# Start order, narrower causal masks and a holding rule in a two-layer attention and feed-forward kernel

## The chip, the cores and the metric

The kernel runs on one core of a Trainium2 chip. The metric is device time in microseconds; three runs of the kernel before gave 1493.4, 1504.54 and 1507.78 us, median 1504.54. The engines are TensorE (PE, with its weight loads as PEld), VectorE (DVE), ScalarE (ACT), GpSimd (POOL) and SyncE (SP), which issues the DMAs.

## The reference

x is 8 batches of 512 tokens with 256 channels; ctx_512 is 8 x 512 x 128. Two layers follow one another. Each has an attention with 16 heads of 16 channels and a quantised feed-forward network of width 1024, and each adds its result to x:

```python
x = x + _L0_xattn_ref(_layernorm(x), ctx_512, ...)   # causal self-attention + cross-attention, one output product
x = x + _L0_ffn_ref(_layernorm(x), ...)              # rmsnorm, 8-bit activations per token, ternary weights, GELU
x = x + _L1_xattn_ref(_layernorm(x), ctx_512, ctx_512, ...)   # cross-attention
x = x + _L1_ffn_ref(_layernorm(x), ...)              # 8-bit activations and weights, one scale per tensor, GELU
```

The causal part is the one that the masks belong to:

```python
att = jnp.einsum('bhqd,bhkd->bhqk', q, k) * scale
causal = jnp.tril(jnp.ones((T, T), bool))
att = jnp.where(causal[None, None], att, -jnp.inf)
y = jnp.einsum('bhqk,bhkd->bhqd', jax.nn.softmax(att, axis=-1), v)
```

## The kernel before

**The work and its tiles.** The attention is cut into 24 units (`UNITS`, L36): for each batch an S unit (causal self-attention), a C unit (cross-attention of layer 0) and an X unit (cross-attention of layer 1). A unit has four groups G of four heads, so there are 96 groups. Every group goes through three series of steps:

- `max_one` (L632): scores with queries on partitions, 48 rows of q and k (three parts, which make up one product with the precision of two) into a pair of PSUM banks; for S units the causal mask is added by `masks` (L615); VectorE takes the row maxima (`mx`).
- `exp_one` (L720): the scores again, with keys on partitions and two more rows (the row maxima, and ones), so that the maximum is already subtracted; for S units again `masks`; ScalarE takes the exponential into a tile `p`.
- `av_part` (L768): p times v into one bank, four heads in four column strips of the array (32 columns each).

In an S unit a score step has one or two query tiles (L49, L51), and each of these has one 128 x 128 block on the diagonal. `masks` adds NEG to what lies above it by two products per array half c (64 rows each), k = 0 and 1: identity times mask for the maxima, mask times identity for the exponentials, each over all 128 columns of a block. For two blocks a product has 256 columns.

**What prepares the groups.** `ln_job` (L477) loads x, takes its statistics on VectorE, normalises it (for the first batch on VectorE, else on GpSimd) and turns it on TensorE into `xlt`. `weights_job` (L414) loads the query and key weights (`raw`) and reorders their columns (`w_Sq`, `w_Sk` and so on); the tag "oc" has two buffers. `prep_job` (L529) multiplies by them; ScalarE adds the bias from `qk_bias` (tile `qkt`), and the high and the low part of each value are split (for n < 2 on VectorE, else on GpSimd). `stack_job` (L566) copies the parts by six DMAs from `qkt` into the stacked rows of `qk`. `rows_job` (L670) turns the maxima into rows, `mrow`, and puts them into `qk` by DMA. `vprep_job` (L586) makes v. `init_job` (L1324) writes the rows of ones into `qk` and the ones that belong to v. `inputs_jobs` (L1350) runs `ln_job` and `ctx_job` in the order of the units.

**The order of the work.** It is set when the program is built. `Plan` (from L78) keeps a clock for each engine, with a cost for each operation: a TensorE product of so many columns by `pe` (L104, 0.008 us + columns/2340), a switch between tile modes by `SWITCH` (0.165). The modes are "rows" (scores, two row halves), "cols" (four column strips: values, projections, transposes) and "full". The main loop (from L1411) knows at each step which of the three series can go on: m (maxima), e (exponentials), a (values). A series is urgent if the backlog that the plan sees on its engine is under `FEED` (L223: in rows mode 9.0 us for VectorE, 2.2 for ScalarE; in cols mode 1.0 and 1.0). Urgent steps come first, then jobs by `run_jobs` (L197), then a value product, then any other step. So in rows mode, as soon as no score step is ready, a value product or a job's product is taken, and TensorE changes its mode. `evacuate` (L368) copies a bank to SBUF by ScalarE, if that ends in the plan no later than on VectorE plus `DVE_HANDICAP` (L228, 0.3 us). All engines then run this order as written, with semaphores; the profile shows what the chip makes of it. The helper lines L241 and L259 record nearly every VectorE and ScalarE operation and every matmul, so groups are told apart by their tiles.

**The start before.** In the program's order SyncE issues the eight DMAs of the doubled identity and mask (L356), the first weight (L421), eight of `qk_bias` (L426), x (L483), six of the rows of ones (L1332), and then the other weights.

Of the kernel before, what the change touches and what calls it, by code (L numbers as in the profile page):

```python
# [7 lines left out]
F32 = mybir.dt.float32  # L8
# [3 lines left out]
AF = mybir.ActivationFunctionType  # L12
# [64 lines left out]
class Plan:  # L77
# [26 lines left out]
    def pe(self, cols, mode="full"):  # L104

        if mode != self.mode:
            self.clock["pe"] += SWITCH
            self.mode = mode
        self.clock["pe"] += 0.008 + cols / 2340
        return self.clock["pe"] + PE_OUT - LAT  # L110

    def would(self, kind, n, *deps):
# [110 lines left out]
FEED = {"rows": (9.0, 2.2), "cols": (1.0, 1.0), "full": (1.4, 1.4)}  # L223
PATIENCE = {"rows": -5.0, "cols": -5.0, "full": -5.0}
GQ, AHEAD = 4, 3
ROW_COLS = 600
H1, H2 = {}, {}
DVE_HANDICAP = 0.3  # L228


class Readers:
# [55 lines left out]
def build(tc, A, out):  # L287
# [57 lines left out]
    with tc.tile_pool(name="start_b", bufs=1) as start:  # L345
        ident_b = start.tile([P, P], BF16, name="ident_b")
        nc.vector.tensor_copy(ident_b, ident)
        mask_b = start.tile([P, P], BF16, name="mask_b")
        nc.gpsimd.memset(mask_b, 0.0)
        nc.gpsimd.affine_select(  # L350
            mask_b, mask_b, pattern=[[-1, P]], compare_op=ALU.is_ge, fill=NEG, base=0, channel_multiplier=1,
        )
        for dst, of in ((ident2, ident_b), (mask2, mask_b)):
            for c in range(2):
                for k in range(2):
                    nc.sync.dma_start(dst[64 * c : 64 * c + 64, k], of[64 * k : 64 * k + 64])  # L356
    qk_bias = wp.tile([P, 6, 2], F32, name="qk_bias")

# [53 lines left out]
        WT[nm] = wp.tile([P, 1 if nm in ("Vc", "Vx") else 2, C], F32, name=f"w_{nm}")  # L412

    def weights_job():  # L414
        b6 = A["qk_bias"].rearrange("(g c d h) i u -> g c h d (i u)", g=2, c=2, h=2)
        for n, nm in enumerate(("Sq", "Sk", "Cq", "Ck", "Xq", "Xk")):
            for u in range(2):
                nk = WT[nm].shape[2]
                yield from take("oc")
                raw = tile("oc", [P, T], F32, f"raw_{nm}{u}")[:, : nk * P]  # L420
                nc.sync.dma_start(raw, WSRC[f"{nm}{u}"])  # L421
                t = dma(64 * nk)
                if n == 0 and u == 0:
                    for c, g, h in ((c, g, h) for c in range(2) for g in range(2) for h in range(2)):
                        p0 = 64 * c + 2 * g + h
                        nc.sync.dma_start(qk_bias[p0 : 64 * c + 64 : 4].rearrange("p i u -> p (i u)"), b6[g, c, h])  # L426
                        dma(6)
                yield t + LAT
                for k in range(nk):
                    for h in range(2):  # L430
                        full = raw[:, k * P : (k + 1) * P].rearrange("p (g c d h) -> p h c d g", g=2, c=2, h=2)
                        dst = WT[nm][:, u, k].rearrange("p (c d g h) -> p h c d g", c=2, g=2, h=2)
                        (nc.vector if n < 2 else nc.gpsimd).tensor_copy(dst[:, h], full[:, h])
                        t = plan.run("dve" if n < 2 else "pool", 0.2)
                give("oc", t)
                at["w", nm, u] = t
            if n == 1:
# [39 lines left out]
    def ln_job(key, src, nm, n_uses):  # L477

        if key[0] == "X":
            yield from until(("x3", key[1]))  # L480
        yield from take("xa")
        x = tile("xa", [P, NT, C], F32, f"xa_{nm}")
        nc.sync.dma_start(x, src())  # L483
        yield dma(512) + LAT
# [44 lines left out]
    def prep_job(n):  # L529
        kind, b = UNITS[n // 2]  # L530
        u = n % 2
        yield from take("qkt")
        tt = tile("qkt", [P, 4, T], F32R, f"qkt{n}")
        tl = []
        for i, (hi, lo) in enumerate(((0, 1), (3, 2))):
            wname, which = KIND[kind][i]
            key, ring = src_key(kind, b, which)
            yield from until(key, ("w", wname, u))
            xs = xlt[key]
            nk = xs.shape[1]  # L540
            ps, pb = yield from gen_bank()
            for k in range(nk):
                yield pe_next()
                wide(ps, WT[wname][:, u, k], xs[:, k, :], k == 0, k == nk - 1)
                tm = plan.pe(4 * T, "cols")
            used(key, ring, tm)
            bias = qk_bias[:, BIDX[wname], u : u + 1]
            full = tt[:, lo, :].bitcast(F32)
            nc.scalar.activation(full, ps, AF.Identity, bias=bias)
            t = op("act", T + 110, tm)  # L550
            give_bank(pb, t)
            yield t + LAT
            if n < 2:
                nc.vector.tensor_copy(tt[:, hi, :], full)
                th = op("dve2", T, t)
                nc.vector.tensor_tensor(tt[:, lo, :], full, tt[:, hi, :].bitcast(F32), ALU.subtract)
                tl.append(op("dve", T))
            else:
                copy_ts(tt[:, hi, :], full)
                th = op("pool", T, t)  # L560
                low_part(tt[:, lo, :], full, tt[:, hi, :])
                tl.append(op("pool2", T, th))
        qkt_t[n] = (tt.bitcast(F32), tl)
        at["qkt", n] = max(tl[0], th)

# [46 lines left out]

    mx_t = {}

    def masks(ps, c, blocks, lhs, rhs):  # L615

        n = len(range(*blocks.indices(NT)))
# [14 lines left out]
    def max_one(s):  # L632
# [21 lines left out]
        if kind == "S":  # L654
# [1 line left out]
            first = size[0] // P - 1  # L656
            step = size[-1] // P
            for c in range(2):
                masks(ps[:, c], c, slice(first, first + (len(qts) - 1) * step + 1, step), ident2, mask2)
# [60 lines left out]
    def exp_one(s):  # L720
# [25 lines left out]
        if kind == "S":  # L746
            step = (T - kts[0] * P) // P
            for c in range(2):
                masks(ps[c], c, slice(0, (len(kts) - 1) * step + 1, step), mask2, ident2)
# [18 lines left out]
    def av_part(s):  # L768
# [7 lines left out]
        for kt in kts:  # L776
            for j in range(4):
# [633 lines left out]
    while plan.jobs or a < len(AV_STEPS):  # L1411
# [279 lines left out]
```

## Time and profile before

| what | value |
|---|---|
| median of three runs | 1504.54 us |
| the profiled execution's own time | 1499.04 us |
| its span, first to last instruction | 1497.3 us |
| mean granted TensorE clock | 0.979 |
| weight loads of score products (two groups) | 152.1 and 146.3 us |
| maxima, all forms x768 | 809.5 us |
| exponentials, all forms x1408 | 715.8 us |
| value products x3072 | 363.9 us |
| mask products of exponentials, of maxima, x768 each | 65.6 and 65.1 us |
| DMA mean rate | 138 GB/s |

The profile's page gives busy times per engine, their course in 40 slices of the span (a digit is the busy share in tenths), the waits, and groups of instructions with count, busy time, mean duration in ns and the idle time before them. The timeline gives start, length, engine, line, operation and count, and in brackets the idle time before an instruction with what ended it. A busy time of TensorE is an envelope over pipelined products, so rates are read from start to start. Idle time of an engine that nothing waits for costs nothing.

### The profile page before, as it was taken

The page shows a single profiled execution, that of the slowest core. Times are in us where ns is not written, and L with a number is a line of the kernel's source. Part 1 is how long each engine was busy: PE and PEld are TensorE (multiplying, and loading weights), DVE is VectorE, ACT ScalarE, POOL GpSimd, SP SyncE. Part 2 cuts the span into 40 slices and gives each one's busy share as a digit, 9 for nine tenths or more (in the row PEclk, how much of TensorE's full clock was granted, in tenths as well). Part 3 has the DMA queues.
Part 4 walks back from the last instruction along what each step waited for, and adds up shares of the span by engine and source line. Part 5 has one row for each costly group of instructions (what it writes and reads, how often), then busy time and mean ns, then how long its engine had stood idle before and what let it go on. Part 6 is the DMA issues. An engine that isn't in the chain of part 4 may idle for free. (4 is left out here: it accounts for less than half of the span.)

```text
span 1497.3 us, 36194 instructions
## 1 busy us (share of the span) xinstructions
PE 1382.0 (92%) x14414; PEld 593.3 (40%) x14416; DVE 1194.1 (80%) x1723; ACT 1023.2 (68%) x1862; POOL 670.6 (45%) x928
## 2 busy tenths in 40 slices
PE   3899999999999999999999999999999989999768
PEld 1443444444433443443344334344333333333427
DVE  2787688788786897798876988698888978894597
ACT  1266667757757767767876677758778767778585
POOL 1552254464462455445634543555355533413237
PEclk9999999999999999999999999999999999999899
DMA  4854565576664666566549564757556656652343
GB/s 112 188 152 97 131 137 123 137 144 170 144 143 107 153 145 129 130 139 155 125 115 164 156 138 104 162 126 175 132 114 162 157 126 174 150 153 95 142 108 113
DMA packets 155612, 207.03 MB, mean 138 GB/s; under 512 B 71940, under 2 KB 74244, under 8 KB 154932
## 3 DMA queue, kind: packets, MB, share of 16 engines
q1 hardware_dynamic: 155444, 204.73, 56.9%
q8 instruction: 113, 1.85, 0.5%
q14 instruction: 55, 0.45, 0.1%
HBM read 68.15 MB, written 47.43 MB: 77 GB/s over the span
## 5 line engine op out<-in xcount | busy, mean ns | idle before, releaser
L241 DVE TENSOR_REDUCE mx<-pair 128x2 f32<-128x1024 f32 (+3 forms) x768 | 809.5, 1084 | 194.0 <-PE pair L259 186.9
L241 ACT ACTIVATE p<-bank 128x512 f32<-128x512 f32 (+1 forms) x1408 | 715.8, 585 | 271.5 <-PE bank L259 265.1
L259 PE MATMUL bank<-p,v 128*32 128x512 f32 (+3 forms) x3072 | 363.9, 551 | 2.6 <-ACT p L241 1.2
L259 PE MATMUL bank<-qk 50*128 50x512 f32 (+3 forms) x1536 | 331.1, 433 | 21.7 <-ACT p L241 9.5
L259 PE MATMUL pair<-qk 48*128 48x512 f32 (+3 forms) x1536 | 322.7, 431 | 24.8 <-DVE mx L241 14.1
L259 PEld LDWEIGHTS bank<-qk 50*128 50x128 f32 x1536 | 152.1, 186 | 279.1 <-ACT p L241 162.2
L259 PEld LDWEIGHTS pair<-qk 48*128 48x128 f32 x1536 | 146.3, 187 | 222.0 <-DVE mx L241 108.3
L366 POOL TENSOR_SCALAR qkt<-qkt 128x512 fp32r<-128x512 f32 x92 | 57.6, 626 | 277.9 <-ACT qkt L241 191.7
L391 POOL TENSOR_TENSOR qkt<-qkt 128x512 fp32r<-128x512 f32 x92 | 117.6, 1279 | 7.7
L241 ACT ACTIVATE qkt<-bank,qk_bias 128x512 f32<-128x512 f32 x96 | 66.5, 693 | 71.0 <-PE bank L259 51.0
L259 PEld LDWEIGHTS bank<-p,v 128*32 128x32 f32 x3072 | 69.8, 109 | 106.8 <-issue 80.2
L847 POOL TENSOR_TENSOR yt<-oc,rb 128x512 f32<-128x512 f32 x31 | 40.0, 1292 | 71.5 <-DMA rb<-scrz 59.1
L259 PE MATMUL bank<-ident,mask 64*128 64x128 bf16 (+1 forms) x768 | 65.6, 240 | 0.0
L259 PE MATMUL pair<-mask,ident 64*128 64x128 bf16 (+1 forms) x768 | 65.1, 243 | 0.0
L241 DVE SCALAR_TENSOR_TENSOR h<-bank,so,bc_l_b 128x512 f32<-128x512 f32 x64 | 45.7, 741 | 3.0 <-PE bank L259 1.4
L241 ACT ACT_TABLE_LOAD x34 | 43.6, 1283 | 3.1 <-DVE h L241 1.7
L1152 POOL TENSOR_SCALAR h<-h,sh 128x1024 f32<-128x1024 f32 x32 | 35.9, 1121 | 20.5 <-DVE sh L241 20.5
L1134 POOL TENSOR_SCALAR ms<-ms 128x2 f32<-128x2 f32 x16 | 3.1, 191 | 93.2 <-ACT jq L241 92.7
L241 ACT COPY ev<-bank 128x512 f32<-128x512 f32 x54 | 32.3, 599 | 14.8 <-PE bank L259 14.7
L395 POOL TENSOR_SCALAR hq<-h 128x1024 bf16<-128x1024 f32 x32 | 33.4, 1044 | 18.5 <-DMA hqt<-hq 13.0
L259 PE MATMUL bank<-l0w,hqt 128*32 128x256 bf16 x1024 | 37.9, 274 | 2.6 <-DMA hqt<-hq 1.7
L1591 POOL TENSOR_SCALAR g<-g,sc_g 128x2048 f32<-128x2048 f32 x11 | 29.4, 2690 | 22.2 <-DVE sc_g L241 22.2
(230 smaller groups left out, 1711.0 us busy)
## 6 DMA issues: line engine op xcount, KB each, us to landing
qk<-qkt SPq DMA_DIRECT2D x288, 256.0 KB
scro<-ev SPq DMA_DIRECT2D x94, 256.0 KB
oc<-scro SPq DMA_DIRECT2D x47, 256.0 KB
rb<-scrz SPq DMA_DIRECT2D x47, 256.0 KB
x_d<-xb SPq DMA_DIRECT2D x15, 512.0 KB
xa_s<-in_x SPq DMA_DIRECT2D x8, 512.0 KB
xb<-in_x SPq DMA_DIRECT2D x8, 512.0 KB
xr<-x_d SPq DMA_DIRECT2D x16, 256.0 KB
```

Of the source, the lines that this page charges most:

```text
L241: r = f(*args, **kw)
L259: r = self.eng.matmul(out, *args, **kw)
L366: nc.gpsimd.tensor_scalar(dst, src, 1.0, 0.0, ALU.mult, ALU.add)
L391: nc.gpsimd.tensor_tensor(dst, full, high.bitcast(F32), ALU.subtract)
L395: nc.gpsimd.tensor_scalar(dst, src, -MAGIC, 1.0, ALU.add, ALU.mult)
L847: nc.gpsimd.tensor_tensor(y, o, rb, ALU.mult)
L1134: nc.gpsimd.tensor_scalar(ms, ms, 1.0 / FF, 1e-5, ALU.mult, ALU.add)
L1152: nc.gpsimd.tensor_scalar(ht, ht, s[:, t - t0 : t - t0 + 1], MAGIC, ALU.mult, ALU.add)
L1591: nc.gpsimd.tensor_scalar(gs, gs, sg[:, 1:2], MAGIC, ALU.mult, ALU.add)
```

## The change

It has five parts.

1. **Start.** The first x and the first halves of Sq and Sk are loaded by the first three DMAs of the program, ahead of the constants. The bias comes next, then the doubled identity and mask. The weights are taken in the order Sq0, Sk0, Sq1, Sk1. The V and output weights, the rows of ones with v's ones, and the inputs of all later units wait until the plan has stacking 0 landed. In preparations 0 and 1 both products are issued before either is split.
2. **Masks.** For the maxima the second product (k = 1) covers columns 64 to 128 only; for the exponentials product k covers columns 64k to 64k + 64 only. The weights of these products stay 64 x 128.
3. **Order rule.** In rows mode, with nothing urgent, the loop looks for an m or e step whose inputs come ready within `LINGER` = 0.2 us; if there is one, the plan's TensorE clock is moved to it, and no value product is taken before.
4. **Evacuations.** `DVE_HANDICAP` goes from 0.3 to 0.8 us.
5. **The plan's costs.** A product in cols mode costs the larger of columns/2415 and columns/2165 - 0.08; mask products and value products have new column counts.

```diff
-        self.clock["pe"] += 0.008 + cols / 2340
+        self.clock["pe"] += max(cols / 2415, cols / 2165 - 0.08) if mode == "cols" else 0.008 + cols / 2340
...
+LINGER = 0.2
...
-DVE_HANDICAP = 0.3
+DVE_HANDICAP = 0.8
...
+    first_x = tile("xa", [P, NT, C], F32, "xa_s0")
+    nc.sync.dma_start(first_x, A["x"][0])
+    at["x0"] = dma(512)
+    heapq.heappop(plan.rings["xa"])
+    first_raw = {}
+    for i, nm in enumerate(("Sq", "Sk")):
+        first_raw[nm] = tile("oc", [P, T], F32, f"raw_{nm}0")
+        heapq.heappop(plan.rings["oc"])
+        nc.sync.dma_start(first_raw[nm][:, :C], A["wa"][2 * i])
+        at["raw", nm] = dma(128)
...
+        order = [(nm, u) for nm in ("Sq", "Sk", "Cq", "Ck", "Xq", "Xk") for u in range(2)]
+        order[:4] = [("Sq", 0), ("Sk", 0), ("Sq", 1), ("Sk", 1)]
...
+            if n == 3:
+                yield from until(("stack", 0))
                 for v in ("Vs", "Vc", "Vx", "Wp", "Wo"):
...
+            ready.append((wname, ps, pb, tm, hi, lo))
+            if n >= 2 or i == 1:
+                for r in ready:
+                    th = yield from split(*r)
+                ready = []
...
         for k in range(2):
+            lhs, rhs = (mask2, ident2) if keys else (ident2, mask2)
+            cols = slice(64 * k, 64 * k + 64 if keys else P)
+            n = len(range(*blocks.indices(NT)))
             nc.tensor.matmul(
-                diag, lhs[rows, k], rhs[rows, k].unsqueeze(1).broadcast_to([64, n, P]), start=False, stop=k == 1
+                diag[:, :, cols], lhs[rows, k], rhs[rows, k, cols].unsqueeze(1).broadcast_to([64, n, cols.stop - cols.start]),
+                start=False, stop=k == 1,
             )
...
-            t = plan.pe(2 * len(qts) * P, mode="rows")
+            t = plan.pe(len(qts) * 192 + 60, mode="rows")
...
-            t = plan.pe(2 * len(kts) * P, mode="rows")
+            t = plan.pe(len(kts) * P + 80, mode="rows")
...
-            t = plan.pe(4 * n + 30, mode="cols")
+            t = plan.pe(4 * n, mode="cols")
...
     def init_job():
+        yield from until(("stack", 0))
...
                 yield from ln_job(("S", b), lambda b=b: A["x"][b], f"s{b}", 7)
+                if b == 0:
+                    yield from until(("stack", 0))
...
-        if plan.run_jobs(0.0 if urgent else ready["a"] - PATIENCE[plan.mode] if can["a"] else None):
-            idle = 0
+        soon = [
+            t + LAT for k in "me" if plan.mode == "rows" and not urgent and (t := ready[k]) is not None
+            and t + LAT < before + LINGER and feed[k] < FEED["rows"]["me".index(k)] and (k == "e" or ahead < LEAD)
+        ]
+        if plan.run_jobs(0.0 if urgent or soon else ready["a"] - PATIENCE[plan.mode] if can["a"] else None):
+            idle = idle + 1 if plan.now == before else 0
...
             continue
+        if soon:
+            plan.clock["pe"] = max(before + 1e-3, min(soon))
+            continue
```

More of the change, by code (lines that the diff above doesn't have):

```diff
@@ L352, in build @@
         )
+        qk_bias = wp.tile([P, 6, 2], F32, name="qk_bias")
+        b6 = A["qk_bias"].rearrange("(g c d h) i u -> g c h d (i u)", g=2, c=2, h=2)
+        for c, g, h in ((c, g, h) for c in range(2) for g in range(2) for h in range(2)):
+            p0 = 64 * c + 2 * g + h
+            nc.sync.dma_start(qk_bias[p0 : 64 * c + 64 : 4].rearrange("p i u -> p (i u)"), b6[g, c, h])
+            dma(6)
         for dst, of in ((ident2, ident_b), (mask2, mask_b)):
@@ L356, in build @@
                     nc.sync.dma_start(dst[64 * c : 64 * c + 64, k], of[64 * k : 64 * k + 64])
-    qk_bias = wp.tile([P, 6, 2], F32, name="qk_bias")
+                    dma(16)
     qk_t = [wp.tile([P, 4, 2, T], F32R, name=f"qk{i}") for i in range(NQK)]
@@ L414, in weights_job @@
     def weights_job():
[L415 to L418, printed above, removed]
+        order = [(nm, u) for nm in ("Sq", "Sk", "Cq", "Ck", "Xq", "Xk") for u in range(2)]
+        order[:4] = [("Sq", 0), ("Sk", 0), ("Sq", 1), ("Sk", 1)]
+        for n, (nm, u) in enumerate(order):
+            nk = WT[nm].shape[2]
+            if n < 2:
+                raw, t = first_raw[nm], at["raw", nm]
+            else:
@@ L419, in weights_job @@
                 yield from take("oc")
-                raw = tile("oc", [P, T], F32, f"raw_{nm}{u}")[:, : nk * P]
-                nc.sync.dma_start(raw, WSRC[f"{nm}{u}"])
+                raw = tile("oc", [P, T], F32, f"raw_{nm}{u}")
+                nc.sync.dma_start(raw[:, : nk * P], WSRC[f"{nm}{u}"])
                 t = dma(64 * nk)
[L423 to L435, printed above, removed]
@@ L436, in weights_job @@
-                at["w", nm, u] = t
-            if n == 1:
+            yield t + LAT
+            for k in range(nk):
+                for h in range(2):
+                    full = raw[:, k * P : (k + 1) * P].rearrange("p (g c d h) -> p h c d g", g=2, c=2, h=2)
+                    dst = WT[nm][:, u, k].rearrange("p (c d g h) -> p h c d g", c=2, g=2, h=2)
+                    (nc.vector if n < 4 else nc.gpsimd).tensor_copy(dst[:, h], full[:, h])
+                    t = plan.run("dve" if n < 4 else "pool", 0.2)
@@ L438, in weights_job @@
+            give("oc", t)
+            at["w", nm, u] = t
+            if n == 3:
+                yield from until(("stack", 0))
                 for v in ("Vs", "Vc", "Vx", "Wp", "Wo"):
@@ L480, in ln_job @@
             yield from until(("x3", key[1]))
[L481 to L484, printed above, removed]
+        if key == ("S", 0):
+            x = first_x
+            yield at["x0"] + LAT
+        else:
+            yield from take("xa")
+            x = tile("xa", [P, NT, C], F32, f"xa_{nm}")
+            nc.sync.dma_start(x, src())
+            yield dma(512) + LAT
         var, neg, r, te = yield from stats(x, nm)
@@ L534, in prep_job, with split @@
         tl = []
[L535 to L547, printed above, removed]
+        def split(wname, ps, pb, tm, hi, lo):
             full = tt[:, lo, :].bitcast(F32)
-            nc.scalar.activation(full, ps, AF.Identity, bias=bias)
+            nc.scalar.activation(full, ps, AF.Identity, bias=qk_bias[:, BIDX[wname], u : u + 1])
             t = op("act", T + 110, tm)
@@ L562, in prep_job @@
                 tl.append(op("pool2", T, th))
+            return th
+        ready = []
+        for i, (hi, lo) in enumerate(((0, 1), (3, 2))):
+            wname, which = KIND[kind][i]
+            key, ring = src_key(kind, b, which)
+            yield from until(key, ("w", wname, u))
+            xs = xlt[key]
+            nk = xs.shape[1]
+            ps, pb = yield from gen_bank()
+            for k in range(nk):
+                yield pe_next()
+                wide(ps, WT[wname][:, u, k], xs[:, k, :], k == 0, k == nk - 1)
+                tm = plan.pe(4 * T, "cols")
+            used(key, ring, tm)
+            ready.append((wname, ps, pb, tm, hi, lo))
+            if n >= 2 or i == 1:
+                for r in ready:
+                    th = yield from split(*r)
+                ready = []
         qkt_t[n] = (tt.bitcast(F32), tl)
@@ L613, in build, with masks @@
     mx_t = {}
-    def masks(ps, c, blocks, lhs, rhs):
-        n = len(range(*blocks.indices(NT)))
+    def masks(ps, c, blocks, keys):
         diag = ps.rearrange("p (a b) -> p a b", b=P)[:, blocks]
@@ L658, in max_one @@
             for c in range(2):
-                masks(ps[:, c], c, slice(first, first + (len(qts) - 1) * step + 1, step), ident2, mask2)
-            t = plan.pe(2 * len(qts) * P, mode="rows")
+                masks(ps[:, c], c, slice(first, first + (len(qts) - 1) * step + 1, step), False)
+            t = plan.pe(len(qts) * 192 + 60, mode="rows")
         for off, w, qt in zip(offs, size, qts):
@@ L748, in exp_one @@
             for c in range(2):
-                masks(ps[c], c, slice(0, (len(kts) - 1) * step + 1, step), mask2, ident2)
-            t = plan.pe(2 * len(kts) * P, mode="rows")
+                masks(ps[c], c, slice(0, (len(kts) - 1) * step + 1, step), True)
+            t = plan.pe(len(kts) * P + 80, mode="rows")
         tm = t
@@ L1422, in build @@
         urgent = [(feed[k], k) for k, f in zip("me", FEED[plan.mode]) if can[k] and feed[k] < f]
-        if plan.run_jobs(0.0 if urgent else ready["a"] - PATIENCE[plan.mode] if can["a"] else None):
-            idle = 0
+        soon = [
[4 more added lines that the diff above has]
+            idle = idle + 1 if plan.now == before else 0
+            assert idle < 20000, (m, e, a)
+            continue
+        if soon:
+            plan.clock["pe"] = max(before + 1e-3, min(soon))
             continue
```

## The prediction

> **What bounds the kernel now.** I read the page's busy times first, then the waits by engine, then the stretches, and last the timeline of the start. Page, part 1, and the row of the matmuls in part 2:
>
> ```profile
> PE 1382.0 (92%) x14414; PEld 593.3 (40%) x14416; DVE 1194.1 (80%) x1723; ACT 1023.2 (68%) x1862; POOL 670.6 (45%) x928
> ...
> PE   3899999999999999999999999999999989999768
> ```
>
> TensorE is full from the second slice to the last but a few; only the start and the tail have room. Who waits for whom (total us, times, longest):
>
> ```profile
> ACT p L241 <- PE bank L259: 265.1, 308, 4.5
> ...
> DVE mx L241 <- PE pair L259: 186.9, 244, 4.7
> ```
>
> The exponentials and the maxima wait for scores. In the other direction TensorE's matmuls stand still for over 20 ns only some 64 us in all between 45 and 1380 us (summed over the timeline). But in those 1335 us VectorE is busy 87 to 90% and ScalarE 75 to 86%, so VectorE is close behind. So a microsecond of TensorE's own work saved there is worth most of a microsecond, not all of it.
>
> The start, by the timeline (start, us, engine, line, count):
>
> ```profile
> 2.01 2.48 SPq L356 DMA_DIRECT2D ident<-ident_b  x4
> ...
> 4.54 2.51 SPq L356 DMA_DIRECT2D mask<-mask_b  x4
> ...
> 7.09 0.73 SPq L421 DMA_DIRECT2D raw_Sq<-in_wa  x1
> 7.86 5.00 SPq L426 DMA_DIRECT2D qk_bias<-in_qk_bias  x8
> ...
> 12.90 0.58 SPq L483 DMA_DIRECT2D xa_s<-in_x  x1
> 13.61 4.34 SPq L1332 DMA_DIRECT2D qk<-ones_rows  x6
> 16.84 1.40 DVE L241 BATCH_NORM_STATS2 st_s<-xa_s 128x6 f32<-128x256 f32 x4 [6.70 <-DMA xa_s<-in_x]
> ...
> 21.57 3.64 PE L259 MATMUL bank<-ident_r,xa_s 128*32 128x128 f32 x64 [21.57 <-DVE xa_s L241]
> ...
> 31.48 4.46 SPq L576 DMA_DIRECT2D qk<-qkt  x6
> ...
> 42.65 0.55 PE L259 MATMUL pair<-qk 48*128 48x128 f32 x3 [0.45 <-DMA qk<-qkt]
> ```
>
> x is issued at 12.90, behind 17 small issues of SyncE (8 constants, one weight, 8 bias); everything up to the first scores at 42.65 hangs on it as one chain.
>
> **Part 1, the start.** After the change x is SyncE's first issue. ScalarE's first instruction starts at 0.74, so I put x at 0.8. Issue to statistics took 16.84 - 12.90 = 3.9 us; two 128 KB weights follow at once, so I allow 0.5 us more: statistics at 5.2. Statistics to first transpose took 21.57 - 16.84 = 4.7: transposes at 9.9, a gain of 11.7. SyncE then issues two weights (1.1 us), bias (5.0), identity and mask (2.5 + 2.5) and the second half's weights (1.1), done by about 14; the second halves land near 16.5, before preparation 1 needs them at about 18. Preparation 0 now multiplies q and k one after the other before either is split; before, k's product stood 0.8 us behind q's evacuation. First stacking issue: 31.48 - 11.7 - 0.8 = 19.0. Stacking to first scores was 11.2 us with 2 MB of other loads in front of it (the V and output weights, one x, one context, issued 21.6 to 25.3). These now wait for the stacking, so I take 10 us: first scores at 29, 13.5 us earlier.
>
> What is paid back: (a) the values' products (36.5 to 41.9, 5.6 us of TensorE) ran while the stacking was in flight; they now follow the first scores, where TensorE is idle 0.2 of 5 us (45:50), 1.0 (50:55), 0.5 (55:60) and 2.3 (60:65): 4 us hidden, 1.6 paid. (b) Held back until stacking 0 lands are five weight issues (2.3 us of SyncE), six of ones (4.3), context, the next x and the next query weights: some 8 us of SyncE's queue and 2 MB, about 10 us at the 200 GB/s of that stretch, with stacking 1 still in flight. Behind them wait the next unit's products (at 46.9 before); the first maxima do not, and 24 score steps of about 1.09 us give VectorE some 26 us of cover. If the cover fails, stacking 2 comes up to 5 us late; I charge 1.5. (c) TensorE now stands idle some 7 us before its first scores. The trace: the first 64 transposes took 3.64 us, later 32 of the same took 1.08 (72.53), so a start after idleness cost 1.5 us; the granted clock stands at 0.50 from 65 to 70, after a stretch with 2.72 busy of 5. [...] Start: -13.5 + 1.6 + 1.5 + 1.4 = **-9** (bounds -13 and -4).
>
> **Part 2, half masks.** 192 score steps and 192 transposed steps of the causal units carry four mask matmuls each (x768 and x768), 128 steps of each kind with one diagonal block and 64 with two. Scores, masks, scores, masks, then values:
>
> ```profile
> 138.24 0.28 PE L259 MATMUL pair<-qk 48*128 48x256 f32 x2
> 138.36 0.12 PEld L259 LDWEIGHTS <-ident 64*128 64x128 bf16 x4 [0.17 <-issue]
> 138.37 0.29 PE L259 MATMUL pair<-mask,ident 64*128 64x128 bf16 x4
> ...
> 138.46 0.38 PE L259 MATMUL pair<-qk 48*128 48x256 f32 x2
> ```
>
> From the first mask to the next work, medians over the timeline: followed by scores 96 ns (one block) and 148 (two); followed by another tile mode[...], 217 and 323. Each kind of follower has about half the steps. When it drains, 106 ns buy 256 columns (the two row halves run side by side): 0.41 ns a column. The change drops 64 (one block) or 128 (two) of the scores' columns and 128 or 256 of the transposed scores': 128 x 27 + 64 x 53 + 128 x 53 + 64 x 106 ns = 20.4 us over all, 10.2 for the drained half. When scores follow, the slope is 52/256 = 0.20 ns: 5 us for that half. Against it: the number of weight loads doesn't fall. [...] The row stands between: four mask loads lie within 0.12 us, but the scores' matmul that starts at 138.46 lasts 0.38 where the same shape at 138.24 lasted 0.28, so it waited for its own load. I give the undrained half 3 of its 5 us: 13 us of TensorE (bounds 3 and 20). VectorE at 87 to 90% takes part of it: three quarters, **-10**.
>
> **Part 3, the order rule.** In rows mode with nothing urgent, the builder now holds TensorE until a score that comes ready within 0.2 us, instead of starting a value product. A value product of eight instructions takes 0.882 us before one of its own mode and 0.996 before scores, so a switch costs 0.114 us; the timeline has 1278 switches, 146 us. 1408 score steps in 637 runs are 2.2 a run. If a third of the runs (200) hold on for 0.1 us: 20 us of standing, and if each adds a step, runs of 2.5 (1408/2.5 = 563) save 74 pairs of switches, 74 x 0.228 = 17 us. The row says even: **0** (bounds -12 and +20). Queued behind the held score on TensorE is the value product, and behind it the freeing of the p tiles. The finer model of column-mode products only shifts the builder's clock by 2 to 5%: 0, bounds -4 and +4.
>
> **Part 4, evacuations.** The handicap goes from 0.3 to 0.8 us. VectorE does 95 of them now:
>
> ```profile
> L241 DVE COPY ev<-bank 128x512 f32<-128x512 f32 x40 | 27.2, 680 | 2.0 <-PE bank L259 1.7
> ...
> L241 DVE COPY v<-bank 128x512 f32<-128x512 f32 x14 | 9.4, 685 | 3.4 <-ACT p L241 2.2 <-PE bank L259 1.0
> ```
>
> and 35 CASTs of row maxima at 0.407. If half move, VectorE loses 0.5 x (27.2 + 9.4 + 14 + 3) = 27 us and ScalarE gains about 24 (0.599 and 0.354 apiece). Neither is the bound, but VectorE is the nearer one: **-2** (bounds -8 and +6; ScalarE at 86% in the last attention stretch, 1010 to 1380, is where it could hurt: an evacuation there stands ahead of exponentials).
>
> **Sum.** -9 - 10 + 0 - 2 = -21 us. The profiled execution took 1499.0 us (span 1497.3, 1.7 around it), so it becomes 1478. The median shown, 1504.54, lies 0.37% above that execution; with the same share, -1.4%, the median becomes **1483 us**.
>
> **Rivals.**
> A. The start and masks pay in full and the order rule saves switches: -13 - 15 - 10 - 4 = -42, 1462 us. For it: ScalarE's 265 us and VectorE's 187 us of waiting for scores. Against: VectorE at 90% leaves little.
> B. The gain is given back: VectorE, not TensorE, sets the pace, so masks bring 3, and the held-back loads cost 5 of the start's gain: -4 - 3 + 0 = -7, 1497 us. For it: stretches of 4.8 to 5.0 of 5 on VectorE from 50 to 65 us. It is also the case that the masks don't do what they say, the weight loads hiding them.
> C. Slower: the holding. At 0.1 us a hold it pays only if it avoids a pair of switches (0.228 us) in 44% of cases. If it comes at the end of 450 of the 637 runs, 0.15 us each, and avoids none, TensorE stands 68 us more; if the scores fed early give back a third, 45 are left: -21 + 45 = +24, 1529 us. At this price (0.10 us net a hold) it decides from 210 holds on, where the -21 is used up; 360 make it slower by 1%. Against it: a held score was going to be needed, and it feeds the engines that wait.
>
> **How the numbers follow.** Forecast 0.44, A 0.22, B 0.20, C 0.14. About 1% is what a measurement of this kernel tells from no change (its three runs spread from 1493.4 to 1507.8). Faster by over 1% (under 1489.5): the forecast mostly (0.40 of its 0.44) and A: 0.62. Within 1%: B and the rest of the forecast, and a little of C: 0.25. Slower by over 1%: 0.13. The range takes in A's centre and B, and leaves out C and A's far end: 1456 to 1506. The forecast alone spans 1472 to 1492.
>
> **What would show it.** Start: x's issue before 1 us, transposes near 10, first scores near 29; if scores come after 36, the stacking's own transfer sets it. Masks: the two mask groups' busy time (65.6 and 65.1 us) falls by 20 to 40 and 10 to 25%, and the intervals drained fall to 160 and 215 (transposed). Order rule: fewer than 1200 switches, with idle time of score matmuls not over 40 us more. Evacuations: VectorE's 95 fall below 60. I am wrong if switches don't fall while TensorE's idle time grows, or if VectorE's waits for scores grow.

## The result, and the profile after

| | before | after |
|---|---|---|
| median | 1503.35 us (20 runs, 1493.40 to 1508.40) | 1512.12 us (20 runs, 1504.38 to 1517.75) |
| ratio | | 1.0064, 95% interval 1.0045 to 1.0082 |
| profiled execution: span, mean granted clock | 1497.3 us, 0.979 | 1508.7 us, 0.956 |
| clock lost, mean over the runs | 36.8 us (the 125 runs made beside e1 to e16) | 70.7 us |

The changed kernel is 0.6% slower, 9 us, where 1483 us were forecast. "Clock lost" is (1 - mean granted clock) x span, from each run's own record; in the clock records of the kernel before and of the changed one every entry is 1.00 or 0.50, so 70.7 us lost are 141 us at half clock.

The rows that answer to those of before. The page's first part, the matmuls' slices and the granted clock (tenths), then the two waits (us in all, times, longest):

```profile
PE 1392.0 (92%) x14416; PEld 610.4 (40%) x14416; DVE 1178.7 (78%) x1687; ACT 1031.8 (68%) x1898; POOL 670.7 (44%) x928
...
PE   4997998999999999999999899998999988999768
...
PEclk8799999999998999989999999998999999999899
```

```profile
ACT p L242 <- PE bank L260: 244.8, 303, 7.6
...
DVE mx L242 <- PE pair L260: 214.6, 257, 8.4
```

VectorE has 15 us less to do and waits 28 us more for scores; ScalarE, with 9 us more to do, waits 20 us less. VectorE's longer wait was one of the two signs that the prediction named for being wrong. The other did not come: the switches of tile mode fell to 1156, from 1284 in the same count of the timeline (the prediction has 1278).

The start (start, us, engine, line, count):

```profile
0.75 0.40 SPq L331 DMA_DIRECT2D xa_s<-in_x  x1
...
10.57 0.66 PE L260 MATMUL bank<-ident_r,xa_s 128*32 128x128 f32 x8 [10.57 <-DVE xa_s L242]
...
21.20 9.00 SPq L608 DMA_DIRECT2D qk<-qkt  x12
...
30.96 0.47 PE L260 MATMUL pair<-qk 48*128 48x128 f32 x1 [7.59 <-DMA qk<-qkt]
...
32.45 0.87 PE L260 MATMUL pair<-qk 48*128 48x128 f32 x3 [1.02 <-issue]
...
33.71 3.08 DVE L242 TENSOR_REDUCE mx<-pair 128x2 f32<-128x256 f32 x5 [8.38 <-PE pair L260]
```

x is issued at 0.75 (0.8 forecast), the transposes start at 10.57 (9.9), the first scores run at 31.0 to 32.5 (29), against 42.65 before. So the start was won. It is gone 40 us later. A unit has 32 maxima: the last one of the first unit still ends 9.7 us ahead of the kernel before, the first one of the second unit 9.6 us behind. In VectorE's timeline of the changed kernel no maximum starts between 64.94 and 87.80 us:

```profile
73.91 0.16 DVE L242 TENSOR_SCALAR l0ws<-bank 128x1 f32<-128x1 f32 x1 [6.01 <-PE bank L260]
...
79.18 0.42 DVE L242 TENSOR_TENSOR bc_l_bp<-bank,bc_l_bp 128x256 f32<-128x256 f32 x1 [4.63 <-PE bank L260]
...
84.60 0.69 DVE L242 COPY ev<-bank 128x512 f32<-128x512 f32 x1 [1.62 <-PE bank L260]
87.80 1.23 DVE L242 TENSOR_REDUCE mx<-pair 128x2 f32<-128x1024 f32 x1 [2.51 <-PE pair L260]
```

The same maximum in the kernel before:

```profile
78.21 1.21 DVE L241 TENSOR_REDUCE mx<-pair 128x2 f32<-128x1024 f32 x1
```

By the count of finished maxima, the first 2% are done at 49.9 us (58.2 before), the first 5% at 99.9 (93.0 before): 8 us ahead have become 7 us behind.

Masks and evacuations, the page's groups and VectorE's `ev` group:

```profile
L260 PE MATMUL pair<-mask,ident 64*128 64x128 bf16 (+2 forms) x768 | 59.7, 231 | 0.0
L260 PE MATMUL bank<-ident,mask 64*128 64x64 bf16 (+1 forms) x768 | 53.9, 208 | 0.0
```

```profile
L242 DVE COPY ev<-bank 128x512 f32<-128x512 f32 x34 | 23.3, 685 | 11.8 <-PE bank L260 11.0 <-ACT p L242 0.3 <-ACT qkt L242 0.2
```

The mask groups of the exponentials and of the maxima fell by 18% and 8%, a little less than forecast (20 to 40% and 10 to 25%). From the first mask to the next work of another tile mode ("drained" in the prediction) it is now 164 ns for one transposed block and 216 for two (160 and 215 forecast). The trace of the kernel before has 1218 changes between rows and cols: at them the next product starts 70 ns (median; 69 to 71 from the 10th to the 90th percentile) before the recorded end of the latest earlier one, so with that work nearly through; within rows mode it starts 223 ns before it (median). The masks of the two row halves start 3 ns apart (median). Up to here nearly every sign that the prediction asked for is there, and the kernel is slower all the same.

### The profile page after: what moved, and what is told of

The parts are those of the page before. It is cut to its first block, busy times and chain, and to the rows that moved or that the text cites. A ratio compares the mean times of both kernels' runs of the same rounds, so it can differ in the third digit from the quotient of the medians.

```text
span 1508.7 us, 36153 instructions
## 1 busy us (share of the span) xinstructions
PE 1392.0 (92%) x14416; PEld 610.4 (40%) x14416; DVE 1178.7 (78%) x1687; ACT 1031.8 (68%) x1898; POOL 670.7 (44%) x928
## 5 line engine op out<-in xcount | busy, mean ns | idle before, releaser
L260 PE MATMUL bank<-qk 50*128 50x512 f32 (+3 forms) x1536 | 346.1, 445 | 27.5 <-ACT p L242 12.7
L260 PE MATMUL bank<-p,v 128*32 128x512 f32 (+3 forms) x3072 | 367.7, 562 | 2.0 <-DVE mx L242 0.7
L260 PE MATMUL pair<-qk 48*128 48x512 f32 (+3 forms) x1536 | 326.4, 441 | 38.3 <-DVE mx L242 17.0
L260 PEld LDWEIGHTS bank<-qk 50*128 50x128 f32 x1536 | 159.9, 191 | 288.8 <-ACT p L242 169.4
L260 PEld LDWEIGHTS pair<-qk 48*128 48x128 f32 x1536 | 149.4, 193 | 224.1 <-DVE mx L242 105.9
L260 PE MATMUL pair<-mask,ident 64*128 64x128 bf16 (+2 forms) x768 | 59.7, 231 | 0.0
L260 PE MATMUL bank<-ident,mask 64*128 64x64 bf16 (+1 forms) x768 | 53.9, 208 | 0.0
L242 ACT COPY v<-bank 128x512 f32<-128x512 f32 x38 | 22.6, 601 | 44.5 <-PE bank L260 44.1
L242 ACT COPY ev<-bank 128x512 f32<-128x512 f32 x60 | 35.6, 593 | 17.1 <-PE bank L260 16.9
L242 DVE TENSOR_REDUCE am<-h 128x1 f32<-128x1024 f32 x32 | 38.6, 1208 | 0.2 <-ACT h L242 0.2
```

What stands on the lines that cost most here:

```text
L242: r = f(*args, **kw)
L260: r = self.eng.matmul(out, *args, **kw)
```

## The experiments

All ratios are against the kernel before on the same chip, with 95% intervals. The times beside them are medians; a ratio is made from all runs and can differ from the quotient of two medians by some 0.2%.

**The start, with and without the held loads.** e1 is the start alone. e2 takes its three holds out:

```diff
-                yield from until(("stack", 0))
                 for v in ("Vs", "Vc", "Vx", "Wp", "Wo"):
...
     def init_job():
-        yield from until(("stack", 0))
...
-                if b == 0:
-                    yield from until(("stack", 0))
```

> The kernel before with the start of the changed one alone (first x and weights ahead of the constants, both products before the split, later loads held back until stacking 0 has landed). Theory H (the held-back loads): the first maxima come 10 us earlier, but the cross unit's stacking comes late, VectorE has next to nothing to do for some 10 us between 70 and 85 us, and the kernel ends 5 to 10 us later than before (1509 to 1513). Theory C (the clock): the start is won and most of it kept, and the loss of the whole change comes from TensorE at half clock later on; this kernel is 5 to 10 us faster (1493 to 1498). Forecast on record: 9 us faster.

> As the start alone, but with none of the three holds on stacking 0: the value weights, the rows of ones and the next inputs are issued as soon as the plan reaches them. Theory H: the 10 us won at the first maxima stay, 6 to 12 us faster than before (1491 to 1497), and 14 to 20 us faster than the start with the holds. Theory C: no different from the start with the holds, within 4 us.

Measured: e1 1524.48 us, 1.0141 [1.0115, 1.0167]; e2 1491.49 us, 0.9933 [0.9909, 0.9957]. The start without its holds beats the kernel before by 10 to 12 us; e1 is 33 us slower than e2. Not all of that is the holds': by finished maxima e1 is 14 us behind e2 at 5%, where the holds act, 6 behind at half, still 4 ahead of the kernel before there, and 27 behind at the end. On VectorE e2 has the order of the kernel before again from 484 us on, e1 not before 1399, so what e1 loses in its second half is most likely its own order's. e6 takes the holds out of the whole change, and e9 frees only the weights in the start. (In e9 the zeros of v's unused columns are written after the first unit's values, so that part of v is lost in its output.)

> The whole change without the three holds on stacking 0. Theory H: the 10 us of the start come back and nothing else changes, 10 to 20 us faster than the changed kernel (1492 to 1502). Theory C: the time at half clock stays over 100 us and it ends within 5 us of before.

> The start alone, with two of the three holds (the rows of ones, the inputs of later units); the weights job is not held, so that the cross unit's query and key weights are loaded and reordered early again. Theory H (it is the late second pair of query weights, 46.8 instead of 36.0 us at issue, that makes the cross unit's stacking late): the stacking of that unit is issued before 55 us again, and most of the 12 us won at the first maxima is still there at 100 us of progress. If it is the held inputs: it stays where the start with all holds was, +9 at 60 us of progress.

Measured: e6 1502.58 us, 1.0008 [0.9987, 1.0029], so the whole change with its holds is 0.56% [0.28, 0.84], 8 us, slower than without; these two kernels differ in order as well, on VectorE up to 1383 us. e9 1495.86 us, 0.9953 [0.9932, 0.9973], again with the order of before from 484 us on: with the weights freed and the other two holds kept, the start's gain is nearly whole. The places are these, SyncE's and GpSimd's rows of the timeline. Changed kernel:

```profile
30.94 0.34 SPq L457 DMA_DIRECT2D w_Vs<-in_wv  x1
...
38.04 0.33 SPq L443 DMA_DIRECT2D raw_Cq<-in_wa  x1
...
46.84 0.43 SPq L443 DMA_DIRECT2D raw_Cq<-in_wa  x1
...
61.85 0.87 POOL L450 COPY w_Cq<-raw_Cq 128x64 f32<-128x64 f32 x4
...
74.00 1.96 SPq L608 DMA_DIRECT2D qk<-qkt  x3
```

Kernel before:

```profile
24.50 0.38 SPq L421 DMA_DIRECT2D raw_Cq<-in_wa  x1
...
35.99 0.73 SPq L421 DMA_DIRECT2D raw_Cq<-in_wa  x1
...
45.12 0.87 POOL L433 COPY w_Cq<-raw_Cq 128x64 f32<-128x64 f32 x4
...
55.66 4.46 SPq L576 DMA_DIRECT2D qk<-qkt  x6
```

e9:

```profile
23.06 0.70 SPq L442 DMA_DIRECT2D raw_Cq<-in_wa  x1
...
54.90 4.41 SPq L606 DMA_DIRECT2D qk<-qkt  x6
```

The held job is not only the five V and output weights: the cross-attention's query weights stand behind them in the same job. GpSimd reorders their second part at 61.85 instead of 45.12, and the first stacking of the cross unit, which is what the maxima need after the first unit, is issued 18 us later (74.00 against 55.66). In e9 it is where it was, and the lead lasts: 5% of the maxima at 81.9 us (11 ahead of before), all of them 10 ahead.

**Is the start's gain its own?** e2 has the order of the kernel before for most of its time, so its gain could hang on that order. So two other orders were made by moving one of the planner's constants by 2 to 3%, alone (e7, e8) and with e2's start (e13, e14):

```diff
-SWITCH = 0.165
+SWITCH = 0.168     # e7, e11, e13; 0.160 in e8, e12, e14
```

> The kernel before with one number of the planner's changed, the cost of a switch 0.168 instead of 0.165 us: the same work, another order from early on. Theory O (an order's luck is worth several us): differs from before by 3 us or more, either way. If the order as such is worth nothing: within 2 us of before.

> As the last, with 0.160 instead of 0.165 us. Theory O: differs from before, and from the kernel with 0.168, by 3 us or more; with these two and before there are three draws of an order, and their spread is what a difference between two kernels of unlike order has to exceed before it means anything.

> The start without its three holds, as in e2, on another order: the planner's switch price 0.168 instead of 0.165, as in e7. Theory that the order decides: e2's gain of 11.5 us was partly the good order that it happened to keep from about 580 us on; with another order the time is anywhere between 1490 and 1530 us, and need not be below e7's 1527. Rival, that the start's microseconds come on top of whatever order follows: about 12 us below e7, so 1515 us, and e14 about 12 below e8, so 1519.

> As e13, with the switch price 0.160 of e8. Order decides: anywhere between 1490 and 1530 us. Rival, the start adds to any order: about 1519 us, 12 below e8's 1531.

| `SWITCH` | kernel before | with e2's start | start's share |
|---|---|---|---|
| 0.165 | 1 | 0.9933 | -0.67% [-0.91, -0.43] |
| 0.168 | 1.0163 [1.0127, 1.0199] | 1.0074 [1.0045, 1.0102] | -0.88% [-1.33, -0.42] |
| 0.160 | 1.0188 [1.0159, 1.0217] | 1.0123 [1.0096, 1.0150] | -0.64% [-1.03, -0.24] |

Two things are shown here. The start brings 0.6 to 0.9% each time, as e13's and e14's rival said. At 0.165 and 0.160 the two kernels compared soon have the same order (on VectorE from 484 and 154 us on), so there the gain is the start's own; at 0.168 the orders stay different up to 1431 us, and that row holds a draw of the order too. And a constant moved by 3 to 5 ns makes the kernel before 25 and 29 us slower. It adds no work: it changes the order, and with the order which engine copies some of the banks (VectorE has 40 of the `ev` copies before, 50 in e7, 44 in e8). Of these three orders the kernel before has the best, and an edit that the planner sees can draw another. The changed kernel with the same constants:

> The changed kernel with the planner's switch cost of 0.168 instead of 0.165 us: another draw of its order. Before went from 1502 to 1527 by the same edit. Theory O (the tuned order of before is a lucky one, and every change of the planner draws anew): this one is within 10 us of the changed kernel (1502 to 1522), below the redrawn kernels of before. If the changed kernel's order is itself a lucky or unlucky one it moves by over 10 us.

> As the last, with 0.160. Before went to 1531 by this edit. Theory O: 1502 to 1522, so that the mean over three orders of the changed kernel is some 8 us or more below the mean over three of before (1520), though its own order is 9 us above the tuned one of before. If the change as such makes the kernel slower: the means differ by +5 us or more the other way.

Measured: e11 1525.50 us, 1.0162 [1.0127, 1.0198]; e12 1509.32 us, 1.0008 [0.9979, 1.0036] (its runs spread from 1495 to 1513 us, mean 1505.75). Over three orders each, the kernel before has 1.000, 1.016 and 1.019, the changed one 1.006, 1.016 and 1.001. The spread of either is larger than the 0.6% between them, and by their means (1.012 and 1.008) it isn't shown that the change itself, apart from the order, makes the kernel slower.

**The other parts alone.** e3 has the half masks with the planner's costs untouched, so with the same order; e4 has only the holding rule; e5 is everything but the start.

```diff
+            lhs, rhs = (mask2, ident2) if keys else (ident2, mask2)
+            cols = slice(64 * k, 64 * k + 64 if keys else P)
```

```diff
+        soon = [
...
+        if plan.run_jobs(0.0 if urgent or soon else ready["a"] - PATIENCE[plan.mode] if can["a"] else None):
```

> The kernel before with the half masks alone, the planner's costs left as they were, so that every engine has the same instructions in the same order and only the mask products are narrower. Forecast on record: 10 us faster (bounds 3 and 20), 1493. Rival W (the weight loads hide it): within 3 us of before. Theory C: the array has less to do while it waits for VectorE all the same, more windows at half clock, 0 to 5 us faster at most with the time at half clock over the 61 us of before.

> The kernel before with the holding rule alone (0.2 us). Forecast on record: even, with some 1130 switches instead of 1278. Theory C: the waits for scores leave the array short of work often enough that the time at half clock goes from 61 us to about 100; 5 to 10 us slower (1509 to 1513). Theory O (any new order costs or brings some us, by how the planner's times miss the chip's): between 5 us faster and 10 slower with the time at half clock unchanged.

> The changed kernel with the start of before: half masks, the holding rule, the handicap of 0.8 and the planner's new costs. Forecast on record for these: 12 us faster (1491). From the runs so far, masks 0 and holding +5: 3 to 8 us slower (1506 to 1511). Since the start with holds measured 21 us slower alone and the whole change 9, a plain sum would give 12 us faster; if it comes out near that, the parts add; if near before, the later order after each start is what differs (Theory O).

Measured: e3 1503.18 us, 0.9999 [0.9983, 1.0015]: the masks bring nothing to the time. On TensorE they do: summed over all mask steps, from the first mask to the next other product, e3 needs some 12 us less than the kernel before (steps over 0.5 us counted as 0.5). Followed by scores, the transposed ones fell from 96 to 70 ns (one block) and from 148 to 95 (two), those of the maxima stayed at 96 and 149. e4 1508.40 us, 1.0030 [1.0013, 1.0048], with 1167 switches: 117 fewer and 4 to 5 us slower, with one draw of a new order in that figure. e5 1506.59 us, 1.0032 [1.0013, 1.0051]. By TensorE's finished columns, masks apart, e5 is 12 us ahead of the kernel before at 600 us, and 4 to 6 behind at the end; it loses that between 800 and 1100. One of the places, by stretches (busy us and counts of PE, PEld, DVE, ACT, POOL; granted clock; DMA share; GB/s):

```profile
875.00:880.00 5.00, 5.00 (x50) 1.93 (x49) 4.72 (x7) 3.79 (x6) 4.23 (x4) 1.00 0.16 51
880.00:885.00 5.00, 2.02 (x10) 0.71 (x8) 4.06 (x5) 4.97 (x7) 0.01 (x1) 0.95 0.30 105
885.00:890.00 5.00, 4.99 (x22) 1.73 (x26) 4.17 (x4) 5.00 (x11) 0.86 (x2) 0.50 0.00 0
```

```profile
881.66 0.50 PE L260 MATMUL pair<-qk 48*128 48x512 f32 x2 [1.19 <-DVE mx L242]
...
884.03 0.49 PE L260 MATMUL bank<-qk 50*128 50x512 f32 x1 [1.65 <-ACT p L242]
```

From 878.4 to 882.9 ScalarE does two table loads and a GELU (1.28 + 1.91 + 1.28 us) ahead of the exponentials. TensorE waits 1.19 us for VectorE's maxima, then 1.65 for the exponentials, and is busy 2.02 of 5 us; then it runs at half clock (0.50 from 885 to 890 us). So this stall is paid twice.

**The masks on top of the start, and the changed kernel without them.** e15 is e2 with e3's masks, e16 the changed kernel with full-width masks in its own order.

> e2's kernel with half-width masks in the same order of instructions: the two parts of the change that do what they say, without a new order. If freed TensorE time is worth nothing while the clock takes it back (e3): the same as e2, 1489 to 1494 us. If the masks pay their 10 us once the start is better: 1481 us.

> The changed kernel with the masks at full width again, its order unchanged (the planner still believes in half masks). If the half masks' 10 us were there and were hidden only by the bad order: 1522 us, 10 above the changed kernel. If they are worth nothing on the chip in either order, as in e3: 1510 to 1514 us. If they cost by tripping the clock: below 1508 us.

Measured: e15 1496.53 us, 0.9955 [0.9932, 0.9979], against e2 +0.22% [-0.11, +0.56]. e16 1518.20 us, 1.0101 [1.0070, 1.0132]: 0.37% [0.01, 0.73] slower than the changed kernel. So the half masks bring nothing in two orders and 0 to 11 us, some 5, in the third.

**The clock.** Where the masks' microseconds went can be looked at in e3, since its order is that of the kernel before. Stretches of the kernel before, then of e3:

```profile
433.40:436.80 3.40, 3.40 (x32) 1.12 (x24) 3.40 (x5) 2.87 (x6) 3.05 (x5) 1.00 1.05 194
436.80:443.60 6.80, 4.46 (x44) 2.09 (x42) 6.23 (x9) 2.17 (x4) 6.54 (x10) 0.93 0.74 130
443.60:450.00 6.40, 6.40 (x58) 2.09 (x56) 4.86 (x5) 2.76 (x5) 6.40 (x7) 0.81 0.65 155
```

```profile
433.40:436.80 3.40, 1.00 (x11) 0.34 (x9) 3.33 (x6) 1.58 (x3) 3.23 (x4) 1.00 0.99 162
436.80:443.60 6.80, 6.71 (x41) 2.58 (x41) 4.12 (x5) 2.23 (x4) 6.71 (x11) 0.50 0.46 108
443.60:450.00 6.40, 6.40 (x68) 2.42 (x66) 5.40 (x6) 2.40 (x5) 3.51 (x4) 1.00 0.41 121
```

```profile
436.89 0.79 PE L259 MATMUL bank<-qk 50*128 50x512 f32 x1 [2.49 <-DVE mx L241]
```

e3 is some 4 us ahead when it comes to 433 us. There TensorE waits 2.5 us at one product of the exponentials (for VectorE's maxima, by the profile; the row above), stands 2.4 of 3.4 us, and the next 6.8 us run at half clock (0.50), with VectorE busy 4.12 of 6.80 where it was 6.23. The kernel before stands 2.3 us a little later (4.46 of 6.80 busy), and then has 3.4 us at half clock. e3's lead is down to 1 us at 500.

Over all runs: within each kernel, a run that loses 1 us more of clock is longer by 0.72 us (slope over all runs of all kernels, each against its own mean; for the 125 runs of the kernel before, to which e17's expectation ascribes the 0.72, it is 0.82, correlation 0.84). With 0.72:

| kernel | clock lost, us | mean time against before, us | of it 0.72 x the clock | rest |
|---|---|---|---|---|
| e3, masks | 46.1 | -0.5 | +6.7 | -7.2 |
| e2, start without holds | 45.0 | -9.7 | +5.9 | -15.6 |
| e4, holding rule | 46.4 | +4.6 | +6.9 | -2.3 |
| changed kernel | 70.7 | +9.1 | +24.4 | -15.3 |

The rests of the masks, the rule and the whole are near what the prediction gave (-10, 0, -21); by this reckoning the clock took the difference. But this is a correlation: the stalls ahead of half clock (2.49 us in e3, 1.19 and 1.65 in e5) cost time of their own, and both are in the 0.72. Three runs tried the clock itself, by products that compute nothing of use. e10 puts 20 and 10 into each of the two waits of the tail (into a free bank), e17 and e18 were to fill the waits of the body in e3 and e15.

```diff
         s = E.tile([P, 3], F32, name=f"sc_{nm}")
+        fill(20)
         all_max(banks[0], col, s[:, 0:1])
+        fill(10)
```

```diff
     def matmul(self, out, *args, **kw):
+        count, self.count = self.count, self.count + 1
+        if count in FILL:
+            self.fill(FILL[count])
```

> The kernel before with 30 products on each of two places of the tail that nothing reads (w1q by w1q into an unused bank): 20 ahead of each maximum over all and 10 behind it, where TensorE stands 5.0 and 2.6 us (4.9 and 3.1 at the second). They lie in time in which it stands anyway. Theory C (windows of 3.4 us with too little work set the clock to half): the two stretches of 10.2 us at half clock at 1408 and 1453 us go away, and the tail gets 2 to 5 us shorter. If the clock doesn't follow the work: no gain, and up to 2 us lost where the filling runs over.

> e3's kernel (half masks, same order) with 152 products of 512 columns that compute nothing of use, some 32 us of them, put in front of 53 products for which TensorE stood waiting over 0.5 us in stretches where it was busy under 0.68 of 3.4 us, between 60 and 1385 us. They write a bank that is free at that place. Theory that the clock takes the masks' gain: the time at half clock between 60 and 1385 us falls by more than half and, at the 0.72 us that a run loses for each us of lost clock (from the spread of the 125 runs of the kernel before), 12 to 18 us fewer of lost clock make it 9 to 13 us faster than e3, so 1490 to 1494 us. Rival, that half clock only goes with stalls and costs little itself: the clock comes up and the time stays at 1500 to 1506 us. If the products get in the way: over 1506.

> e15's kernel (the start without holds, half masks, same order) with 138 such products, 29 us, at 47 places found in its own trace in the same way. Clock theory: 10 to 15 us fewer of lost clock, 7 to 11 us faster than e15, so 1485 to 1490 us, the fastest of all. Rival: 1494 to 1499, as e15.

e10: 1499.97 us, 0.9983 [0.9967, 0.9999]; clock lost 25.9 us. Stretches of the tail, the kernel before and then e10:

```profile
1408.00:1419.00 11.00, 6.61 (x16) 2.60 (x18) 9.84 (x17) 5.80 (x9) 6.48 (x5) 0.53 0.67 236
...
1453.00:1464.00 11.00, 4.82 (x24) 3.35 (x25) 9.75 (x13) 5.30 (x5) 6.68 (x3) 0.53 0.00 0
```

```profile
1408.00:1419.00 11.00, 8.38 (x37) 3.49 (x36) 10.12 (x19) 5.33 (x8) 6.50 (x5) 1.00 0.67 245
...
1453.00:1464.00 11.00, 8.72 (x51) 4.79 (x50) 10.05 (x13) 6.29 (x6) 5.21 (x2) 1.00 0.00 0
```

With the added products the granted clock goes from 0.53 to 1.00 in both stretches: here the clock follows the work. It bought little, 11 us of clock for 2 to 5 us. VectorE is busy 9.8 of 11 us in these stretches before and 10.1 after, so it is the likelier bound there.

e17: 1521.77 us, 1.0108 [1.0077, 1.0139], clock lost 49.2. e18: 1502.38 us, 0.9993 [0.9966, 1.0021], clock lost 48.1. Both missed what they were made for: the places were counted in the records of the trace, and one product of the program can leave more than one record (the 1536 value products of the kernel before, 4 heads by 4 key tiles in 96 groups, stand as 3072), so the fillers stand elsewhere. In the timeline 63 of 152 and 80 of 138 ran; TensorE didn't stand before any group of them, and the product behind each starts at once, so no wait was filled. What e17 measures is added work: 17 us at 22 places, from the first filler to the next product, cost 16 us [11, 22] against e3. In e18 20 us at 25 places cost 6 us [0, 11] against e15, with 8 us less of clock lost. That a higher clock alone makes the body faster is not shown.

## Why the prediction was wrong

*The start, -9.* Right in size where it was worked out, wrong in what is paid back. The chain came as forecast to within 2 to 3.5 us, and the start without holds measures -10 to -12. "(b) Held back" was charged at 1.5 us, and "if the cover fails, stacking 2 comes up to 5 us late". Stacking 2 came 18 us late, and the maxima fell from 10 us ahead to 10 behind; in the end the changed kernel is 8 us slower than without its holds, with another order in that figure. The step listed "the next query weights" among the held loads, and took 26 us of cover from 24 score steps, but it added up volume (8 us of queue, 10 us of transfer) and did not follow the one small load to its end: `raw_Cq` at 46.84, reorder on GpSimd at 61.85, products, bias, split, stacking at 74.00. The cover ended with the maximum that starts at 64.94.

*(c), the cold clock, 1.4.* No run shows this term of 1.4 us by itself. In its place the changed kernel shows TensorE at half clock from 28.0 to 48.4 us, 20.48 us in one stretch; in the six sixths of it (3.41 us each) its busy shares were 0.12, 0.66, 0.80, 0.87, 0.95 and 1.00. The price was near the 1.4 all the same: the first scores are 11.7 us ahead, the first maximum 9.8 and the last of the unit 9.7, so some 2 us were lost. VectorE was then the busier (4.78 of 5 us from 38 to 43, TensorE 4.36).

*Masks, -10.* This term was mis-sized: 0 in e3 [-2.6, +2.3 us], +3 in e15 [-2, +8], -6 by e16 [-11, 0]. TensorE's own saving is there: some 12 us in e3, 10 in e15 and 11 by e16, where 13 were forecast. So what failed is the step from TensorE's time to the kernel's, "VectorE at 87 to 90% takes part of it: three quarters": nothing came through in two orders, about half in the third. The stretches of e3 from 433 us show what stood against it there: TensorE busy 1.00 of 3.40 us, the longest gap 2.49 us, and half clock for the 6.80 after it. The prediction used the clock for one place in the start, and held it constant elsewhere.

*Order rule, 0.* Within its bounds (-12, +20): e4 is 4 to 5 us slower. The switches fell as forecast (117 fewer in e4, which by the prediction's own 0.114 us is 13 us less). Where these went is not shown: in e4 VectorE's waits for scores grew by 8.5 us and ScalarE's fell by 13.8.

*The planner's costs, "0, bounds -4 and +4".* This is the step that failed in kind. It asked what the new costs do to the clock of the plan, and not that any of them draws a new order. New orders from a constant 2 to 3% away cost the kernel before 25 and 29 us, and move the changed one by +13 and -3 us (medians; +15 and -8 by the ratios). No bound of 4 us could hold that, and none of the rivals was about it. The order rule, the new start and the handicap draw new orders too, and no part has a term for that. That the order drawn was worse than the old one was chance; that there was a draw could be foreseen.

*Evacuations, -2.* Not measured alone. VectorE's evacuations fell as forecast (36 fewer instructions on VectorE, 36 more on ScalarE); e5, which has them with the masks and the rule, is no faster than e4.

*The rivals.* C, slower, was right in sign by luck: it put 45 us on the holding rule, and e4 is 4 to 5 us slower. B named the held-back loads (5 us) and that VectorE's pace leaves little of the masks (3); both are seen.

*The sum.* The start's 11 us and at most 5 of the masks are there; the holds take 8 back. From before to after it is +9, so by subtraction 12 to 17 us are left for the new order with its rule and evacuations. e5 gives 5 to 10 for the same parts. These do not add up to a microsecond, and with orders that differ by 25 us they need not. That a new order can cost this much is shown; that it cost it here is argued from the remainder. Open is also how much of the 12 to 17 is the clock itself and how much the stalls ahead of it.

The best version measured is e2: the first operands ahead, nothing held, all else as before, 0.9933 [0.9909, 0.9957], 1491.49 us.

## What to carry to other kernels

Where a builder orders the instructions, first measure what a meaningless change of one of its constants does; a part that is judged by one build is judged with the draw of an order on top, so try it in the same order or in several, and look in the trace whether the order really is the same. When loads are held back, follow the smallest of them to the stage that needs it: what counts is not the volume but who stands behind it in the same queue or job. Where TensorE waits for other engines, look what becomes of the work it is saved: in e3, some 4 us ahead at 433 us, there was a gap of 2.49 us with 6.80 us at half clock (0.50) behind it, and 12 us saved on TensorE were worth nothing in e3's time (-2.6 to +2.3 us).

## What the runs showed of the hardware

In the clock records of the kernel before and of the changed one every stretch at half clock, but for the last of the run, is 3.41, 6.83, 10.24 or 20.48 us long, so once, twice, three or six times 3.41. The traces of three kernels (before, changed, e3), cut into windows of that length, by TensorE's busy share as the profile has it: the clock fell after 46 windows with shares of 0.00 to 0.86, half of them under 0.52. It stayed full after 1164, of which 99% had over 0.62. It came back after windows of 0.85 to 1.00, nearly all of them at 1.00, but windows of 0.88 to 1.00 also failed to bring it back, 16 of them. So here the clock was lost behind windows that were up to 0.86 busy, and one window at 1.00 did not always regain it: the kernels before and after, both with TensorE 92% busy, lost 37 and 71 us of clock. The busy share is an envelope over pipelined products, so no threshold is read from it.
